# Group norm, keys and values of the next sequence inside the convolution, and weight transforms spread over attention, in a float32 attention-and-convolution kernel

## The chip, the cores and the metric

One core of one Trainium2 chip. The metric is device microseconds (us) of the whole program, the median of a kernel's runs. Engines: PE is TensorE, DVE is VectorE, ACT is ScalarE, POOL is GpSimd. A line number such as L311 belongs to the kernel whose profile is shown.

## The reference

Two layers over an input of 4 x 128 x 64 x 64 in float32. Only the first is touched by the change:

```python
def conv_layer(x):                       # x: (4, 128, 64, 64), each image is one "sequence"
    x = group_norm(x, 32)                # no scale, no shift
    g, theta, phi = conv1x1(x, gw, gb), conv1x1(x, tw, tb), conv1x1(x, pw, pb)   # 64 channels each
    f = einsum('bcn,bcm->bnm', theta, phi) / sqrt(64)                          # 4096 x 4096 per image
    out = conv1x1(einsum('bcm,bnm->bcn', g, softmax(f)), ow, ob) + x
    return relu(conv7x7(x) + conv5x5(x) + conv3x3(x) + out + x)
# x = x + conv_layer(x); the second layer (selective scan both ways, then a recurrence) follows
```

## The kernel before

For each of the four sequences the kernel does the following, one after the other: statistics and group norm; queries, keys and values; attention; a convolution in which the 7x7, 5x5 and 3x3 kernels are merged into one and applied along the rows by a polynomial transform with four pairs of points. `strip` sums on VectorE prepare the transformed input (14 ahead of the first pair, six more for each of the three later points), TensorE multiplies with transformed weights `u`, VectorE combines each pair of products into the outputs. The 128 x 128 `gmean` product averages statistics over the channels of a group, so a norm costs a small chain: mean product, subtraction, variance product, reciprocal root on GpSimd, and a product for the key bias.

```python
nc.vector.tensor_reduce(bsum, bias, AX.X, ALU.add)          # the first thing asked of VectorE
...
for b in range(B):
    for j in range(NQ):
        nc.vector.bn_stats(st[:, j, :], tb[:, bass.ts(j, NC)])
    nc.vector.bn_aggr(mv, st)
    nc.tensor.matmul(pm, k.gmean, mv[:, 0:1], ...)           # mean of the group
    ...                                                      # gm, dm, qv on VectorE
    nc.tensor.matmul(pv, k.gmean, qv, ...)                   # variance of the group
    ...                                                      # rs on GpSimd, xp = (t - gm) * rs on VectorE
    for q in range(NQ):                                      # 8 blocks of 512 columns
        nc.tensor.matmul(pt, tw2, xp[:, rows, 3 : W + 3], ...)
        nc.vector.tensor_scalar(theta[:, bass.ts(q, NC)], pt, tb2, None, ALU.add)   # queries
        nc.tensor.matmul(pp, pw2, xp[:, rows, 3 : W + 3], ...)                      # keys
        ...
    # attention: 128 steps (8 blocks of 16): 2 score products, exp on ScalarE,
    # one addition to the denominator on VectorE, 2 value products
    if b == 0:
        ...conv_weights(...)                                 # the weight transforms
    for n, p in enumerate(POINTS):                           # 4 points, 2 products each, 2 halves
        ...                                                  # strip sums f (strided), xs = f0 +- p * f1
        for q in range(H // QR):
            pr = ps_f.tile(...)                              # two PSUM buffers
            for i in range(2):
                product(pr[:, i], 2 + 2 * n + i, xs[i], q)
            nc.scalar.copy(m, pr[:, 1])
            nc.vector.tensor_tensor(v, pr[:, 0], m, ALU.subtract)
            nc.vector.tensor_tensor(m, pr[:, 0], m, ALU.add)
            ...                                              # four more into the outputs
    # residual on VectorE
```

A scheduler sets the order of the instructions on each engine when the kernel is built. `InOrder` pins an instruction behind the one traced before it; what is not pinned goes where the scheduler finds it ready.

## Time and profile before

| | |
|---|---|
| median time | 3404.35 us (3396.66 to 3410.28, 3 runs) |
| span of the profiled run, granted clock | 3408.1 us, 0.949 |
| PE / DVE / ACT busy | 89% / 79% / 51% of the span |
| end of the first layer (last convolution product) | 1771.9 us |

I use three marks: the first score product of a sequence, the end of its plain 1x1 products (they open the convolution's pairs), and the last product of the first layer. From the 1x1 products to the next first score is called a **transition** below; it takes 135.9, 135.5 and 135.5 us here. From the first score to the 1x1 products is the **attention stretch**: 330.4 us in the first sequence and 292.8 in the three others.

The page's slices of the span show where PE is not full, and two of its groups (columns: line, engine, operation, output from input, forms, count; then busy us and mean ns; then idle us of the engine just before, and what ended most of it).

```profile
PE   5899989999899998999986889888988898888776
PEclk9999989999899999999997998899899999999888
...
L289 PE MATMUL pr<-x,u 128*128 128x512 f32 x896 | 386.3, 593 | 0.0
...
L301 DVE SCALAR_TENSOR_TENSOR f<-xp,f 128x1120 f32<-128x1120 f32 x88 | 192.0, 2192 | 1.0
```

The left half of the slices is the first layer: nines, with a dip at the start and at each transition. The products of the pairs (L289) never wait: 0.0 us idle ahead of 896 instructions.

### The profile page before, as it was taken

What the parts mean: (1) busy time and instruction counts of PE and PEld (TensorE: products, weight loads), DVE (VectorE), ACT (ScalarE), POOL (GpSimd) and SP (SyncE); (2) the same over time, 40 slices, a digit from 0 to 9 for tenths busy, and PEclk for the clock granted to TensorE, in tenths of its full rate; (3) what the DMA queues carried; (4) which work ended last, traced back from release to release, by engine and by line L of the source; (5) the groups of instructions that cost most, each with busy time, mean ns of one, the idle gap of its engine ahead of it and who ended that gap; (6) DMA issues with size and microseconds to landing.
All of it is one profiled execution on the core that took longest, in us unless ns stands there. A gap on an engine that the chain in (4) does not pass through costs nothing.

```text
span 3408.1 us, 44290 instructions
## 1 busy us (share of the span) xinstructions
PE 3021.9 (89%) x16048; PEld 1456.4 (43%) x16048; DVE 2692.6 (79%) x4528; ACT 1740.2 (51%) x3087; POOL 528.1 (15%) x735
## 2 busy tenths in 40 slices
PE   5899989999899998999986889888988898888776
PEld 2223333333333333333344556555655565555446
DVE  6987767778677786877856998898889888898755
ACT  2444104441044420444205776777677767777454
POOL 0000000000000000000001433243324332333310
PEclk9999989999899999999997998899899999999888
DMA  4000000000000000000002322322223333333002
GB/s 149 17 1 1 0 0 1 1 1 0 0 1 1 0 0 0 1 1 1 1 11 59 75 82 68 78 75 76 74 77 76 75 75 78 82 81 81 3 1 100
DMA packets 72004, 128.21 MB, mean 38 GB/s; under 512 B 16864, under 2 KB 19936, under 8 KB 70880
## 3 DMA queue, kind: packets, MB, share of 16 engines
q1 hardware_dynamic: 65696, 120.84, 13.3%
q10 hardware_dynamic: 6080, 4.44, 0.4%
q8 instruction: 129, 2.11, 0.3%
q14 instruction: 99, 0.81, 0.1%
HBM read 115.80 MB, written 9.44 MB: 37 GB/s over the span
## 4 chain that ended last, share of the span: by engine, by line
PE 55%; DVE 28%; ACT 5%; issue 4%; POOL 3%; DMA 3%; SPq 0%; ACTq 0%; DVEq 0%; POOLq 0%
PE pf L91 13%; PE acc L91 12%; PE pr L289 11%; DVE xx L763 6%; PE pc L289 3%; DVE bc L763 3%; DVE cbc L849 2%; ACT xx L91 2%; DVE y L886 2%; DVE xdd L842 2%; DVE xdt L842 2%; DMA cbc<-csd 2%; DVE den L233 1%; PE pys L866 1%; PE pj L901 1%
## 5 line engine op out<-in xcount | busy, mean ns | idle before, releaser
L229 ACT ACTIVATE ex<-pf 128x1024 f32<-128x1024 f32 x512 | 497.7, 1021 | 493.6 <-PE pf L91 462.9
L233 DVE TENSOR_TENSOR den<-den,ex 128x1024 f32<-128x1024 f32 x448 | 547.6, 1222 | 194.1 <-ACT ex L229 171.3
L91 PE MATMUL pf<-theta,phi 64*128 64x512 f32 x2048 | 517.3, 622 | 26.1 <-ACT ex L229 26.1
L91 PE MATMUL acc<-ex,gT 128*64 128x512 f32 x2048 | 505.3, 610 | 0.0
L289 PE MATMUL pr<-x,u 128*128 128x512 f32 x896 | 386.3, 593 | 0.0
L91 PEld LDWEIGHTS pf<-theta,phi 64*128 64x128 f32 x2048 | 176.0, 187 | 359.9 <-ACT ex L229 218.8
L91 ACT ACTIVATE cbc<-cbc,s 128x128 f32<-128x128 f32 x1024 | 312.9, 406 | 0.0
L91 PEld LDWEIGHTS acc<-ex,gT 128*64 128x64 f32 x2048 | 122.7, 136 | 348.3 <-issue 346.4
L289 PEld LDWEIGHTS pr<-x,u 128*128 128x128 f32 x896 | 170.0, 190 | 219.3 <-issue 216.0
L763 DVE SCALAR_TENSOR_TENSOR xx<-pj,cw,xx 128x509 f32<-128x509 f32 (+2 forms) x384 | 259.6, 736 | 0.4
L866 PE MATMUL pys<-cbc,xdt 128*64 128x128 f32 x2048 | 185.1, 302 | 81.5 <-DVE y L886 81.3
L91 POOL TENSOR_TENSOR rms<-rms,neghalf 128x2 f32<-128x2 f32 x128 | 113.0, 883 | 583.7 <-DVE rms L912 583.7
L330 ACT COPY m<-pr 128x512 f32<-128x512 f32 x32 | 18.7, 586 | 356.5 <-PE pr L289 356.5
L301 DVE SCALAR_TENSOR_TENSOR f<-xp,f 128x1120 f32<-128x1120 f32 x88 | 192.0, 2192 | 1.0
L91 ACT ACTIVATE cbc<-cbc 128x1536 f32<-128x1536 f32 x128 | 190.0, 1484 | 3.4
L91 POOL TENSOR_TENSOR y<-y,zs 128x512 f32<-128x512 f32 x128 | 163.3, 1276 | 147.3 <-DVE y L886 144.0
L866 PEld LDWEIGHTS pys<-cbc,xdt 128*64 128x64 f32 x2048 | 118.9, 145 | 148.0 <-DVE y L886 111.3
L776 PE MATMUL pj<-un,full 128*128 128x512 f32 x256 | 150.6, 695 | 33.3 <-DVE xx L763 18.3
L754 PE MATMUL pj<-un,full 128*128 128x512 f32 x256 | 147.9, 663 | 34.9 <-DVE xx L763 20.2
L91 ACT ACTIVATE xx<-pj,cb,cw 128x512 f32<-128x512 f32 x128 | 97.5, 773 | 148.5 <-DVE y L886 116.5
L177 POOL MEMSET xp<- 128x210 f32 x4 | 1.1, 273 | 1039.9 <-DVE f L301 1039.9
L901 PEld LDWEIGHTS pj<-wout,y 128*128 128x128 f32 x1024 | 133.4, 200 | 58.7 <-issue 46.7
(210 smaller groups left out, 4997.3 us busy)
## 6 DMA issues: line engine op xcount, KB each, us to landing
cbc<-csd SPq DMA_DIRECT2D x256, 256.0 KB, 4.3
cbc<-csd SPq DMA_DIRECT2D x256, 128.0 KB, 4.5
t<-in_x SPq DMA_DIRECT2D x3, 2048.0 KB, 12.1
out<-t SPq DMA_DIRECT2D x2, 2048.0 KB, 18.2
out<-t ACTq DMA_DIRECT2D x2, 2048.0 KB, 18.3
w<-in_w7t SPq DMA_DIRECT2D x3, 896.0 KB, 5.0
t<-in_x SPq DMA_DIRECT2D x4, 512.0 KB, 4.9
v<-in_w5t SPq DMA_DIRECT2D x2, 640.0 KB, 4.0
```

What stands on the lines that cost most here:

```text
L91: return self.tc.keep_in_program_order(getattr(self.engine, name)(*args, **kw))
L229: nc.scalar.activation(ex, pf, AF.Exp, scale=scale)
L233: nc.vector.tensor_tensor(den[q], exs[q, 0] if m == 1 else den[q], ex, ALU.add)
L289: nc.tensor.matmul(o, u[:, n, y, :], x[:, q * QR + y : q * QR + y + QR, :], start=(y == 0), stop=(y == 6 and odd is None),)
L301: nc.vector.scalar_tensor_tensor(f, strip(i + 2 * j), cs[j], f, ALU.mult, ALU.add)
L754: pe.matmul(pp, full[:, d, DI + h * P : DI + (h + 1) * P], own(un, d, g), start=True, stop=True)
L763: vec.scalar_tensor_tensor(x[:, o:], self.pp[i][:, 0 : MG - o], cw[:, i, tap : tap + 1], x[:, o:], ALU.mult, ALU.add)
L776: pe.matmul(pz, full[:, d, h * P : (h + 1) * P], cols, start=True, stop=True)
L842: vec.tensor_tensor(x, px, self.r[f][:, :, self.c, :].unsqueeze(3).to_broadcast(heads), ALU.mult)
L849: vec.tensor_tensor(self.lt, self.lt, self.gm.unsqueeze(2).to_broadcast([P, ND, NHEAD, P]), ALU.mult)
L866: pe.matmul(o, self.xdt[:, d, h, :], self.lt[:, d, h, :], start=True, stop=S is None)
L901: pe.matmul(po[:, bass.ts(d, P)], self.y[:, d, h, :], wout[:, d, h, :], start=(h == 0), stop=(h == 1))
```

## The change

Its intent: fill the gaps between sequences and the ragged first attention. (1) The sum of the biases moves from the very start to behind the first attention. (2) The weight transforms become a generator, one step of which is taken per attention step. (3) The next sequence's statistics are issued ahead of the pairs of the convolution, its norm, keys and values inside the last pair, the first half of its queries behind the first half of the last pair, and the second half inside its attention. (4) Queries are evicted by ScalarE instead of VectorE.

```diff
-        nc.vector.tensor_reduce(bsum, bias, AX.X, ALU.add)
-        ...                                       # matmul with gb, add
-        pe = InOrder(tc, nc.tensor)
+        pe, vec = InOrder(tc, nc.tensor), InOrder(tc, nc.vector)
...
-                nc.vector.bn_stats(st[:, j, :], tb[:, bass.ts(j, NC)])
+                vec.bn_stats(st[:, j, :], t[:, ds(b * T + j * NC, NC)])
...
-                nc.vector.tensor_scalar(theta[:, bass.ts(q, NC)], pt, tb2, None, ALU.add)
+                nc.scalar.activation(theta[:, bass.ts(q, NC)], pt, AF.Identity, bias=tb2)
...
-                    nc.vector.tensor_tensor(den[q], exs[q, 0] if m == 1 else den[q], ex, ALU.add)
+                    vec.tensor_tensor(den[q], exs[q, 0] if m == 1 else den[q], ex, ALU.add)
+                next(beside, None)                # one step of the weight transforms
...
+                if n == NT // 4:
+                    theta += [queries(xp, h) for h in range(1, NH)]
...
+            after = statistics(b + 1) if b + 1 < B else None
             for n, p in enumerate(POINTS):
...
+                last = n == len(POINTS) - 1
+                if last and after:
+                    gm, rs, km = after
+                    xp = normalise(b + 1, gm, rs)
+                    phi, gT = keys(xp, km)
                 for h in range(NH):
...
+                    if last:
+                        ...                       # residual of this half
+                        if after and h == 0:
+                            theta = [queries(xp, 0), theta[1]]
...
+            for _ in range(32):
+                next(weights)
+            ...
+            attention(0, xp, theta, phi, gT, vec, weights)
+        vec.tensor_reduce(bsum, bias, AX.X, ALU.add)
```

Small parts left out here: the division of a block is split into three steps at different places, the check on the denominators takes sums by ScalarE instead of a maximum by VectorE, and the inputs of the later sequences are requested behind the first weights.

## The prediction

> **What bounds the kernel now.** I read the page's slices first: TensorE (PE) is at 89% of the span, and the convolution layer, which alone is changed, ends near 1772 us. Then the table of busy time by stretch, for layer 0 (columns: stretch, its length, busy us and instructions of PE, weight loads, VectorE, ScalarE, GpSimd, then granted clock, DMA share, GB/s).
>
> ```profile
> 61.80:486.60 424.80, 399.45 (x1342) 134.35 (x1338) 341.21 (x358) 149.07 (x178) 0.94 (x4) 0.98 0.03 8
> 530.40:915.20 384.80, 384.56 (x1330) 132.79 (x1330) 277.54 (x226) 136.55 (x142) 0.94 (x4) 1.00 0.00 1
> ...
> 915.09:956.38 41.29, 24.45 (x168) 10.87 (x166) 40.81 (x37) 9.84 (x20) 0.55 (x1) 0.79 0.00 1
> ```
>
> A sequence from its first score product to its last convolution product is PE bound: 384.6 of 384.8 us at clock 1.00. Three places are not. The first sequence takes 424.8 us for the same work (A). It starts only at 61.8 us (B). Between sequences lie 41.29 us (C), three times, in which VectorE is busy 40.81 us. The timelines say why. B: VectorE runs in order, and the first thing asked of it is the sum of four tiny biases.
>
> ```profile
> 12.08 0.69 DVE L158 BATCH_NORM_STATS2 st<-t 128x6 f32<-128x512 f32 x1 [1.50 <-DMA t<-in_x]
> ...
> 29.94 0.16 DVE L146 TENSOR_REDUCE bsum<-bias 128x1 f32<-128x4 f32 x1 [17.05 <-DMA bias<-in_ob]
> ...
> 33.99 2.42 DVE L181 TENSOR_SCALAR xp<-t,gm,rs 128x4096 f32<-128x4096 f32 x1 [0.76 <-POOL rs L80]
> ...
> 61.82 1.99 PE L91 MATMUL pf<-theta,phi 64*128 64x512 f32 x8
> ```
>
> C: the queries' evictions (0.75 us) stand in VectorE's order between strip sums (2.17 us), and PE waits for each.
>
> ```profile
> 932.89 2.17 DVE L301 SCALAR_TENSOR_TENSOR f<-xp,f 128x1120 f32<-128x1120 f32 x1
> 933.05 0.50 PEld L201 LDWEIGHTS pt<-xp,tw 128*128 128x128 f32 x2 [4.29 <-DVE theta L202]
> 933.05 2.08 PE L201 MATMUL pt<-xp,tw 128*128 128x512 f32 x2 [2.72 <-DVE theta L202]
> ```
>
> A: the weight transforms and 14 strip sums stand between the additions to the denominator; ScalarE waits for these additions (its buffers come free by them) and PE for ScalarE.
>
> ```profile
> 151.67 1.29 DVE L233 TENSOR_TENSOR den<-den,ex 128x1024 f32<-128x1024 f32 x1
> 152.80 2.22 DVE L301 SCALAR_TENSOR_TENSOR f<-xp,f 128x1120 f32<-128x1120 f32 x1
> 153.05 1.02 ACT L229 ACTIVATE ex<-pf 128x1024 f32<-128x1024 f32 x1 [2.19 <-PE pf L91]
> 154.13 2.08 PE L91 MATMUL pf<-theta,phi 64*128 64x512 f32 x4 [1.13 <-ACT ex L229]
> ```
>
> [...] 0.50 from 920 to 935 us inside gap C, 1.00 once dense; [...] after waits of 2.2 and 3.1 us near 123 and 102 us eight products took 3.66 and 3.50 us instead of 1.94. [...] Here the last bias took 18.3 us to land while 8 MB of input were under way.
>
> **The change, part by part.** Unit times from the trace: a convolution product (two records) 0.858 us, a step of attention 1.92 us of PE (4+4 records of 0.24), a denominator addition 1.17 us from start to start, a strip sum 2.12, an x combination 1.25, a reciprocal 3.26, one statistics instruction 0.63, a post-processing of one pair of products 5.4 (two of 0.7, four of about 1.0), a weight step 0.35 (five in 1.76).
>
> *Start.* The bias sum moves behind the first attention. The last input piece lands at 12.1; two statistics to 13.4; the chain that took 3.26 us (30.73 to 33.99) and one 0.2 us operation more bring the normalisation to 17.0, and 2.4 more to 19.4 (36.4 before). Eight key products with two ScalarE evictions of 0.48 each and some weight scalings between them pace at about 1.3 us[...]: 32; values 4 to 35; four query products 38.7. The first score product comes 23.1 us earlier. VectorE does its first 32 weight steps (about 12 us) in this shadow. In the built order the later inputs are requested behind the first weights, the third weight block near 32 us, so I expect it by 38, before it is needed near 43.
>
> *First attention.* Removed: the clump of weight steps. By the built order about 90 of them lie one per attention step: per 16 steps VectorE needs 15x1.17 + 0.6 + 3.26 + 0.6 + 15.5x0.35 = 27.4 us, PE 16x1.92 + 0.86 = 31.6. That fits; I allow 5 us of hiccups, since ScalarE's scalings wait for VectorE in order. But then, as the strip buffers open when the weight buffers close, the order puts 14 strip sums and 8 statistics between 15 denominator additions, in the sixth and seventh query block: 14x2.12 + 8x0.63 + 15x1.15 + 2x3.26 + 2 = 60 us of VectorE for 31.6 of PE. Four exp buffers cover about 4 us, so some 24 to 25 us of PE wait remain. Four query products are moved in: 3.4 us and 2 for ScalarE to evict them. Sum 5 + 25 + 5.4 = 35.4, against the 37.6 lost now (424.8 less 387.2, the latter with first products included). Gain 2.2.
>
> *Each transition.* On PE nothing goes away: 8 key, 8 query products and the values, 17.7 us, move into the last products or the next attention. The idle part of gap C is 41.3 - 17.7 = 23.6. What takes its place? VectorE's strip sums must still be done, and the order shows where. (1) A tiny product for the variance stands two products after the convolution's 1x1 part, but its operand is made after all strips: PE gets there at 821.8 on the old time axis, VectorE at 826.8. 5 us, 0.9 for the small products, 1.5 for half clock. (2) The next sequence's 14 strip sums (29.7 us) now lie between the post-processings, six of them in one block of 12.7 us before the third and again before the fifth. Two PSUM buffers: PE may begin pair k+2 only when VectorE has read pair k. Laying both orders side by side from pair 1 at 838.5: pair 5 waits 2.3, pair 6 1.2, pair 7 4.4: 8 us. (3) Queries wait for the first half's outputs: 1.5 us; values' evictions 1. So the next first score product is at 947.2 instead of 956.4, 9.2 earlier. (4) It pays 3.4 for the four queries moved into attention and about 3.5 because their eviction on ScalarE waits for the second half to be finished. Net 2.3, three times: 7.
>
> *Small ones.* The row maximum (0.68) leaves VectorE for a ScalarE copy with sum, 8 query evictions also; neither engine bounds attention (1.02 of 1.92 on ScalarE). The second layer's order on VectorE is unchanged: no effect.
>
> *Sum.* 23 + 2 + 7 = 32 us of 3404: about 3372. Since every piece of my reading that is uncertain was rounded to the dear side, I say 3366.
>
> **The rivals.** First, the intent comes off: PE never starves, transitions lose 23.6 each less about 5, attention of the first sequence all of its 37.6: 23 + 33 + 56 = 112, so 3292. For it: VectorE's mean is only 277.5 of 384.8 us, so there is room for 30 us more per sequence if it is spread well. Against: the order is fixed when built, and strip sums are clumped where their buffers come free. Second, the gap closes but returns as waits on two PSUM buffers and on the variance product (my reading), 3366. Third, worse: these waits of 4 to 5 us each drop the clock for several us and first attention, with ScalarE waiting for VectorE and VectorE for ScalarE, loses 20 us more: 3400 or slightly above. The clock after gap C stayed at half for some 10 us, which speaks for it; that PE stays mostly busy between these short waits speaks against.
>
> **Range and chances.** Start is sure to about 3 us. First attention may be off by 15 to either side, each transition by 5, three times the same way. That gives 3335 to 3390. Runs of before spread by 14. Faster by over 2% means below 3336: it needs most of rival one, 0.15. Slower by over 2% needs every transition to lose 20 us: 0.03.
>
> **What would show it.** Right if: the first score product lies near 39 us; a stretch of some 60 us late in the first attention has VectorE at 100% and PE at half, with strips between denominator additions; in each convolution a wait of about 5 us for the variance product, then waits of products for VectorE's subtraction or addition of an earlier pair; sequences repeat at about 426 us where they took 428.3. Wrong if: the repeat is under 415 (waits 1 and 2 absent), or the first sequence shows PE above 95% (strips harmless), or the first score product is later than 45 us (a weight or input transfer holds ScalarE).

No term of the sum goes with them: it stays at 23 + 2 + 7 = 32 us, so 3372, given as 3366. Two parts that concern the clock are estimates. The 32 us at which the key products end has some 2 us for a slow beginning (19.4 + 8 x 1.3 is 29.8): in the kernel before, the first three products of 512 columns behind the norm (at 36.97, 38.81 and 40.52 us) took 2.05, 1.91 and 1.63 us and later ones 1.04 to 1.15. That the clock is the cause there is not shown; the granted clock reads 1.00 from 36 to 42 us. The 1.5 us for half clock are near what a slow stretch took from eight records in the kernel before: 1.56 us at 103.4 and 1.67 at 123.6 (score records usually take 1.99).

What the kernel before shows of the rest, by its timeline and its table by stretch: VectorE held to its order at the start, as the eighth statistics instruction, whose input had landed by 12.1 us, ran at 30.01 behind the bias sum (at 11.66 in e1, where that sum is moved). The 0.50 and 1.00 of gap C are granted clock: 0.50 from 920 to 935 us, around and behind PE's wait of 9.67 us and with PE at work from 926.1, and 1.00 from 940 us on, where waits of 0.6 to 0.74 us remain. Behind the wait of 3.12 us at 102.3 it was 0.50 to 0.57 from 103.4 to 106.8, behind 2.21 us at 123.6 it was 0.50 to 0.55 up to 127.2, and 1.00 after each. ScalarE's wait for a denominator addition was 4.38 us at 149.84, and PE's wait for ScalarE behind it 2.41. From 0 to 30 us, while the last bias was landing, the DMA share was 0.88 at 319 GB/s.

## The result, and the profile after

| | before | after |
|---|---|---|
| median of the same rounds | 3407.32 us (3396.66 to 3415.02, 4 runs) | 3362.19 us (3355.72 to 3369.16, 4 runs) |
| ratio | | 0.987, 95% interval 0.9836 to 0.9905 |
| span of the profiled run, clock | 3408.1 us, 0.949 | 3367.4 us, 0.948 |
| end of the first layer | 1771.9 us | 1725.8 us |

A ratio is the mean time of one kernel's runs over that of the other's of the same rounds, so not quite the ratio of the medians. The change is faster by 1.3%, within 2%. The first layer lost 46.1 us; the second one, whose instructions keep their order, took 1636.2 us of the one span and 1641.6 of the other. Over all kernels below that rest lies between 1624.6 and 1641.6 us, with no relation to the edits that I can see. So the end of the first layer is the sharper measure, and I judge by it.

Start and first attention after, from the timeline and from the table by stretch (columns of the timeline: start, us, engine, line, operation, count, and in brackets the idle time before it and what ended it; the table's columns are those that the prediction names).

```profile
16.35 2.41 DVE L185 TENSOR_SCALAR xp<-t,gm,rs 128x4096 f32<-128x4096 f32 x1
...
38.78 1.99 PE L91 MATMUL pf<-theta,phi 64*128 64x512 f32 x8
```

```profile
38.80:230.00 191.20, 184.90 (x755) 55.95 (x754) 148.18 (x188) 103.22 (x132) 0.00 (x0) 1.00 0.02 6
230.00:290.00 60.00, 45.05 (x164) 12.61 (x162) 59.59 (x46) 20.64 (x23) 0.00 (x0) 0.89 0.00 0
370.45:484.95 114.50, 107.54 (x367) 48.32 (x365) 82.34 (x80) 17.77 (x32) 0.60 (x2) 0.99 0.00 0
786.20:911.87 125.67, 114.35 (x376) 51.47 (x374) 86.80 (x83) 17.37 (x32) 1.49 (x5) 0.96 0.00 0
1212.90:1332.24 119.34, 112.31 (x376) 50.84 (x375) 82.28 (x74) 17.60 (x32) 1.49 (x5) 0.97 0.00 0
```

The norm is applied at 16.4 us instead of 34.0, the first score comes at 38.8 instead of 61.8. The weight transforms hardly disturb attention up to 230 us (PE busy 184.9 of 191.2). Then come 60 us with VectorE full and PE at 45.05: strip sums and statistics among the denominators. The last three rows are the transitions, and the surprise is in their lengths: three transitions of the same code differ by up to 11 us. About 5 of them are only a shift: 17 records of the pairs (the profile lists a float32 product as two: the 448 products of the pairs are its 896 records) lie ahead of the first transition, five ahead of the others, and twelve at 0.43 us are 5.1. The PE waits tell the rest. First the products for the variance of the next sequence, PE and then VectorE:

```profile
371.55 0.28 PE L166 MATMUL pv<-qv,gmean 128*128 128x1 f32 x2
791.35 0.59 PE L166 MATMUL pv<-qv,gmean 128*128 128x1 f32 x2 [4.53 <-DVE qv L164]
1218.33 0.59 PE L166 MATMUL pv<-qv,gmean 128*128 128x1 f32 x2 [4.58 <-DVE qv L164]
```

```profile
786.44 4.34 DVE L300 SCALAR_TENSOR_TENSOR f<-xp,f 128x1120 f32<-128x1120 f32 x2
790.70 0.15 DVE L160 COPY gm<-pm 128x1 f32<-128x1 f32 x1
...
791.08 0.22 DVE L164 SCALAR_TENSOR_TENSOR qv<-dm,mv 128x1 f32<-128x1 f32 x1
```

In the second and third transition the 0.15 us copy of the mean stands behind the last strip sums, which end near 790.7; PE has been waiting since 786.8. In the first transition the strip sums were done during the long first attention, so nothing waits. Second, the pairs:

```profile
444.27 1.83 PE L311 MATMUL pr<-x,u 128*128 128x512 f32 x2 [3.93 <-DVE m L354]
...
871.22 2.04 PE L311 MATMUL pr<-x,u 128*128 128x512 f32 x2 [3.96 <-DVE m L354]
...
1267.40 24.27 PE L311 MATMUL pr<-x,u 128*128 128x512 f32 x56 [0.70 <-ACT m L351]
```

```profile
845.52 4.94 DVE L91 BATCH_NORM_STATS2 st<-t 128x6 f32<-128x512 f32 x8
```

A wait of about 3.9 us stands in the first two transitions (with 0.7 and 0.4 us in two earlier pairs) and not in the third, where 0.70 is the only one. At 845.5 us VectorE makes eight statistics between two pairs. They are those of the sequence after the next, brought forward by the scheduler, and the six strip sums of the predicted clump (856.9 to 869.5 us) come behind them; in the third transition there is no such sequence any more, and with its strip sums alone PE waits 0.70 us. The page sums it up, where the group showed 0.0 idle before:

```profile
L311 PE MATMUL pr<-x,u 128*128 128x512 f32 x896 | 398.8, 601 | 10.9 <-DVE m L354 8.7
```

The books of the first layer, by first score products (us):

| kernel | first score | sequence 1 to 2 | 2 to 3 | 3 to 4 | 4th to end | end of layer | median of program | ratio to before, 95% |
|---|---|---|---|---|---|---|---|---|
| before | 61.8 | 466.3 | 428.3 | 428.3 | 387.2 | 1771.9 | 3407.32 | |
| after | 38.8 | 446.2 | 426.9 | 420.4 | 393.6 | 1725.8 | 3362.19 | 0.987 (0.9836, 0.9905) |
| e1_bias_late | 43.4 | 466.4 | 429.0 | 428.2 | 387.2 | 1754.2 | 3395.52 | 0.9973 (0.9952, 0.9995) |
| e2_queries_scalar | 60.0 | 460.6 | 421.8 | 421.3 | 387.2 | 1750.8 | 3390.77 | 0.9957 (0.9937, 0.9977) |
| e9_two_lines | 42.5 | 462.5 | 421.4 | 421.9 | 387.2 | 1735.4 | 3374.78 | 0.9898 (0.9875, 0.9921) |
| e3_old_transition | 37.8 | 456.4 | 435.4 | 433.6 | 396.2 | 1759.5 | 3390.04 | 0.996 (0.9941, 0.9978) |
| e11_unfolded | 38.4 | 447.5 | 425.8 | 417.6 | 391.1 | 1720.4 | 3359.54 | 0.986 (0.9834, 0.9886) |
| e4_few_strips_first | 37.9 | 434.6 | 425.8 | 419.8 | 393.6 | 1711.7 | 3349.02 | 0.9844 (0.982, 0.9869) |
| e5_stats_early | 38.5 | 440.0 | 417.5 | 417.6 | 395.2 | 1708.8 | 3347.96 | 0.9814 (0.9785, 0.9843) |
| e6_strips_beside | 37.7 | 440.2 | 422.2 | 422.9 | 395.8 | 1718.8 | 3358.41 | 0.9848 (0.9819, 0.9877) |
| e7_both | 38.0 | 440.5 | 419.5 | 420.4 | 397.5 | 1715.8 | 3354.09 | 0.9836 (0.98, 0.9873) |
| e8_first_spread | 37.8 | 443.3 | 422.5 | 420.5 | 395.9 | 1719.9 | 3355.18 | 0.9839 (0.9806, 0.9871) |
| e10_chain_spread | 38.5 | 441.4 | 412.8 | 412.8 | 393.6 | 1699.1 | 3335.33 | 0.978 (0.9761, 0.9799) |
| e12_first_too | 38.5 | 450.1 | 414.4 | 412.7 | 393.6 | 1709.3 | 3341.96 | 0.9802 (0.9779, 0.9825) |

Medians come from different chips; the ratios are against the kernel before on the same chip. The end of the layer is read from one profiled run of each kernel. Of the program times that were expected below, all but e10's were too low, by 2 to 33 us. All runs gave correct results but e4.

### The profile page after: what moved, and what is told of

The parts are those of the page before. It is cut to its first block, busy times and chain, and to the rows that moved or that the text cites. A ratio compares the mean times of both kernels' runs of the same rounds, so it can differ in the third digit from the quotient of the medians.

```text
span 3367.4 us, 44357 instructions
## 1 busy us (share of the span) xinstructions
PE 3030.2 (90%) x16048; PEld 1468.6 (44%) x16048; DVE 2652.3 (79%) x4464; ACT 1784.1 (53%) x3183; POOL 529.7 (16%) x735
## 4 chain that ended last, share of the span: by engine, by line
PE 50%; DVE 34%; ACT 5%; issue 5%; POOL 3%; DMA 1%; SPq 0%; DVEq 0%; POOLq 0%; ACTq 0%
PE pf L91 12%; PE acc L91 12%; PE pr L311 8%; DVE xx L846 5%; DVE bc L846 3%; DVE f L300 3%; DVE cbc L932 2%; DVE den L91 2%; ACT xx L91 2%; DVE y L969 2%; DVE xdt L925 2%; DVE xdd L925 2%; PE pj L753 1%; DVE f L298 1%; DVE theta L358 1%
## 5 line engine op out<-in xcount | busy, mean ns | idle before, releaser
L311 PE MATMUL pr<-x,u 128*128 128x512 f32 x896 | 398.8, 601 | 10.9 <-DVE m L354 8.7
L837 PE MATMUL pj<-un,full 128*128 128x512 f32 x256 | 149.8, 670 | 31.8 <-DVE xx L846 19.9
## 6 DMA issues: line engine op xcount, KB each, us to landing
out<-t SPq DMA_DIRECT2D x2, 2048.0 KB, 18.4
```

The lines of the kernel that those rows point to most:

```text
L311: nc.tensor.matmul(o, u[:, n, y, :], x[:, h * QR + y : h * QR + y + QR, :], start=(y == 0), stop=(y == 6 and att is None),)
L837: pe.matmul(pp, full[:, d, DI + h * P : DI + (h + 1) * P], own(un, d, g), start=True, stop=True)
```

## The experiments

The theory after reading the traces: the start gains because a wait for a late transfer leaves VectorE's order; the transitions gain what VectorE no longer does there, and give some of it back as waits on small things that stand behind long ones in VectorE's order. The main rival: the place of the products, inside the convolution, is what gains.

### Parts of the change put into the kernel before

**e1_bias_late**, the bias sum alone:

```diff
-        nc.vector.tensor_reduce(bsum, bias, AX.X, ALU.add)      # at the start, with its product and addition
+            (the same three instructions behind the attention of sequence 0, VectorE's two pinned there)
```

> The kernel before with one edit: the sum of the biases is issued behind the first attention. My theory, that the wait for the bias transfers alone held VectorE back at the start: the first score product moves from 61.8 us to between 43 and 46 (the queries are still evicted by VectorE, so not quite the 38.8 of the changed kernel), the rest of the layer stays as before (repeats of 428.4 us), and the time is about 3390 us, 17 us under the kernel before. The rival, that the start gained because keys and queries were taken off VectorE and regrouped: the first score product stays within 5 us of 61.8 and the time within 6 us of the kernel before.

The first score moved to 43.4 us, 18.4 earlier, and the layer's end by 17.7; later repeats stayed at 428 to 429. For the start the theory stands. The program's time fell by only 7.9 us in the same rounds (3403.41 to 3395.52), not by 17; behind the layer this kernel's profiled run took 1641.5 us and that of the kernel before 1636.2, and the rest of the difference stays open. The 4.6 us from here to the changed kernel's 38.8 are what its other edits at the start give.

**e2_queries_scalar**, the queries' eviction alone:

```diff
-                nc.vector.tensor_scalar(theta[:, bass.ts(q, NC)], pt, tb2, None, ALU.add)
+                nc.scalar.activation(theta[:, bass.ts(q, NC)], pt, AF.Identity, bias=tb2)
```

> The kernel before with one edit: ScalarE adds the bias to the queries and evicts them, instead of VectorE; nothing is moved into the convolution. My theory, that part of what a transition gained is simply work taken off VectorE, which is busy 40.8 of the 41.3 us between the last product of the convolution and the first score product: the stretch from the end of the 1x1 products to the next first score product falls from 135.8 to about 128 us, three times, and the time to about 3383 us. The rival, that only the move into the products gains: that stretch stays within 2 us of 135.8 and the time within 6 us of the kernel before.

Transitions fell to 128.8, 129.0 and 128.5 us, 6.5 to 7.1 each, and the layer's end by 21.1 (the program's time by 12.6 in the same rounds, from 3403.41 to 3390.77). Before and with this line, the end of a transition on PE:

```profile
944.22 1.14 PE L201 MATMUL pt<-xp,tw 128*128 128x512 f32 x2 [0.72 <-DVE theta L202]
...
952.50 3.95 PE L215 MATMUL pg<-gw,xp 128*64 128x64 f32 x128 [0.74 <-DVE theta L202]
```

```profile
936.04 1.04 PE L201 MATMUL pt<-xp,tw 128*128 128x512 f32 x2
937.24 1.14 PE L204 MATMUL pp<-xp,pw 128*128 128x512 f32 x2 [0.17 <-ACT phi L207]
938.32 4.13 PE L215 MATMUL pg<-gw,xp 128*64 128x64 f32 x128
```

The waits of 0.7 us for VectorE, one per block of queries, are gone. The strip sums stay on VectorE, and PE no longer waits for it behind them.

The largest wait of a transition is another one, and this line leaves it. In the kernel before PE waits 16.8 us in all from the last 1x1 product to the next first score, and 9.7 of them at the product for the key bias, whose operand `mx` stands behind the last combinations, the norm and the residual on VectorE (9.65 us in e2). In the changed kernel the whole chain comes early. Before, then after:

```profile
926.11 0.59 PE L190 MATMUL pk<-mx,pw 128*128 128x1 f32 x2 [9.67 <-DVE mx L188]
```

```profile
373.00 0.35 PE L174 MATMUL pk<-mx,pw 128*128 128x1 f32 x2 [0.21 <-DVE mx L172]
```

**e9_two_lines**, both edits together:

```diff
+ (the edits of e1 and e2)
```

> The kernel before with two small edits and none of the reordering: the bias sum behind the first attention, and the queries evicted by ScalarE. The two runs with one edit each took 17.6 and 21 us off the end of the layer (1771.9 us). Theory, that the two add up and that the rest of the change is about even by itself: first score product at 40 to 43 us, transitions 129 us, attentions 293 us, end of the layer at 1729 to 1736 us against 1725.8 of the changed kernel, the time about 3370 us. The rival, that they share a gain: end of the layer at 1745 us or later.

The layer ended at 1735.4 us, 36.5 of the change's 46.1 us, and inside the expected band; the program took 3374.78, a little above the 3370 expected. Two edits of a line or so carry four fifths of what the whole change gains in this layer. The remaining 9.6 us are the sum of gains and losses that the next runs separate.

### Parts of the change taken back

**e3_old_transition**: norm, keys and first queries back behind the convolution.

```diff
-            after = statistics(b + 1) if b + 1 < B else None
+            after = None
...
+                gm, rs, km = statistics(b)       # in the loop, behind convolve of b - 1
+                xp = normalise(b, gm, rs)
+                phi, gT = keys(xp, km)
+                theta = [queries(xp, 0)]
```

> The changed kernel with normalise, keys and the first half of the queries back behind the convolution, and everything else (start, weights beside attention, queries by halves on ScalarE) as changed. If the move into the last products is what gained: the stretch from the 1x1 products to the next first score product goes back to 132 us or more, the sum of a transition and an attention to about 428, and the time to about 3386 us. My theory, that the move is nearly paid back by the waits it makes and the work put behind the first scores: the sum of a transition and an attention is 421 to 425 us (mean of the changed kernel 420.3, before 428.4), and the time 3366 to 3376 us.

My numbers were missed: 1759.5 us, and transition and attention stretch together took 429.5 to 433.8 us, more than before the change. But the edit did more than I meant. The statistics are pinned in the changed kernel, so that once they stood behind the residual, PE waited for them:

```profile
905.74 0.59 PE L158 MATMUL pm<-mv,gmean 128*128 128x1 f32 x2 [13.76 <-DVE mv L156]
...
911.01 6.34 PE L198 MATMUL pp<-xp,pw 128*128 128x512 f32 x8 [1.74 <-DVE xp L185]
```

So the run agrees in its size with the rival and yet does not test it. It shows the cost of statistics at the wrong place.

**e11_unfolded**: only the products go back; statistics and norm stay inside the convolution.

```diff
-                if last and after:
-                    gm, rs, km = after
-                    xp = normalise(b + 1, gm, rs)
-                    phi, gT = keys(xp, km)
...
-                        if after and h == 0:
-                            theta = [queries(xp, 0), theta[1]]
+            if after:                             # behind all pairs
+                gm, rs, km = after
+                xp = normalise(b + 1, gm, rs)
+                phi, gT = keys(xp, km)
+                return xp, [queries(xp, 0)], phi, gT
```

The normalising has no pin, and the built order still has it inside the convolution on VectorE.

> The changed kernel with only the products of the keys, the values and the first queries put back behind the products of the convolution on TensorE; the statistics and the normalising stay inside the convolution. The earlier run that put all of it back also put the statistics behind the residual, which made the mean product wait 13.8 us, so it was no fair test. Theory, that what the fold gains is that the normalised input is ready early, and not that the products stand between others: transitions within 4 us of the changed kernel's 114.3, 126.1 and 119.6, end of the layer at 1724 to 1738 us. The rival, that the place of the products is the gain: each transition 8 us or more longer, end of the layer at 1750 us or later.

The layer ended at 1720.4 us, below the expected band and 5.4 earlier than with the products inside. Transitions grew by 1.3 to 3.1 us (115.6, 129.2, 121.0), attention stretches shrank by 2.6 to 4.2 (to 296.6). Behind the last pair PE goes on without a wait:

```profile
895.27 1.92 PE L198 MATMUL pp<-xp,pw 128*128 128x512 f32 x4
897.35 6.50 PE L198 MATMUL pp<-xp,pw 128*128 128x512 f32 x12 [0.16 <-ACT phi L201]
903.90 4.00 PE L209 MATMUL pg<-gw,xp 128*64 128x64 f32 x128
```

So the rival falls: the place of the products inside the convolution gains nothing. That statistics and norm are made early, so that the normalised input is ready when the last pair ends, is enough.

### The waits that the change made

**e5_stats_early**: the next sequence's statistics beside the attention of sequences 1 and 2 (counted from 0), one per three attention steps; the small chain follows at once.

```diff
-            after = statistics(b + 1) if b + 1 < B else None
+            if b == 0:
+                after = statistics(1)
...
+        def beside(b, xp, box, made):
+            for _ in range(24):
+                yield
+            if b + 1 < B:
+                yield from every(3, statistics_steps(b + 1, box))
```

> The changed kernel with the statistics of the next sequence made one by one beside the attention, in sequences 1 and 2 (sequence 0 as it is). Theory: the 4.5 us wait for the variance product comes from the small chain of the statistics standing behind strip sums on VectorE, and the 3.9 us wait in the seventh pair from eight statistics placed among the pairs; both vanish. Transitions of 114.5, 126.2 and 119.7 us become about 110, 114 and 112; attention stays at 299 to 301; the time falls by about 23 us to 3339. The rival, that the next wait in line (strip sums on VectorE) takes over: transitions shrink by less than 2 us each and the time stays within 6 us of 3362.

Both waits vanished, and the transitions were 107.9, 112.0 and 111.9 us, within 2.1 of what was expected. But the attention stretches of these two sequences grew from 300.8 to 305.5 and 305.7, so the layer ended at 1708.8 and not at 1703. The timeline shows where:

```profile
579.00 0.38 PE L167 MATMUL pv<-qv,gmean 128*128 128x1 f32 x2 [0.86 <-DVE qv L165]
580.51 0.59 PE L175 MATMUL pk<-mx,pw 128*128 128x1 f32 x2 [1.14 <-DVE mx L173]
581.03 2.08 PE L91 MATMUL pf<-theta,phi 64*128 64x512 f32 x4
```

The three one-column products stand in PE's order, each waits for the link before it on another engine, and behind them four score records take 2.08 us instead of 1.13. From 570 to 590 us the granted clock was 0.83. The query block in which this happens took 37.9 us in one sequence and 36.4 in the next, where all its neighbours took 31.5.

**e10_chain_spread**: the same, with the chain's links three attention steps apart and pinned there.

```diff
             pm = ps_c.tile([P, 1], F32, tag="c", name="pm")
-            nc.tensor.matmul(pm, k.gmean, mv[:, 0:1], start=True, stop=True)
+            pe.matmul(pm, k.gmean, mv[:, 0:1], start=True, stop=True)
+            yield
             gm = wk.tile([P, 1], F32, tag="gm", name="gm")
...
+            (a yield between all further links as well)
```

> The run with early statistics, with the small chain of each statistics (mean, variance, reciprocal root, key bias: three products of one column on TensorE, and the small steps between them) spread over the attention, three attention steps between two links, so that no product of the chain waits for VectorE or GpSimd. Theory: of the 4.8 us that each attention grew in that run, the chain's waits and the half clock behind them are all but the eight statistics; attentions of sequences 1 and 2 go from 305.6 back to 300 to 302, transitions stay at 108, 112 and 112, the end of the layer comes at 1698 to 1702 us instead of 1708.8, the time about 3338. The rival, that the statistics' own 5 us of VectorE time is the cost: the attentions stay at 305.

Attention stretches of 300.9, transitions of 107.8, 111.9 and 111.9, end of the layer at 1699.1: all as the theory said. One reservation: the two query blocks that hold statistics and chain still took 31.8 and 32.9 us, 1.7 more than usual. The stretch is not longer than the changed kernel's because its first denominator product came 45.8 us behind the first score and not 47.4: the records behind its wait of 1.78 us at 903.2 took their usual 1.13 and 1.94 us, where those behind 1.76 us in the changed kernel took 2.04 and 2.67. Spreading and pinning were not tried apart. One wait of the chain is left, and the clock of its surroundings is 1.00 (the second line is the stretch of 40 us around it):

```profile
597.30 0.38 PE L91 MATMUL pv<-qv,gmean 128*128 128x1 f32 x2 [0.53 <-DVE qv L91]
```

```profile
590.00:630.00 40.00, 39.47 (x165) 12.36 (x166) 30.11 (x29) 20.06 (x24) 1.53 (x1) 1.00 0.00 1
```

With 3335.33 us and a ratio of 0.978 (0.9761 to 0.9799) this version beats both kernels.

**e6_strips_beside**: the 14 opening strip sums of sequences 1 to 3 spread over attention, statistics as in the change.

```diff
-                attention(b, xp, theta, phi, gT, nc.vector, iter(()))
+                attention(b, xp, theta, phi, gT, vec, beside(b, xp, box, made))
...
+            yield from every(5, first_strips(xp, made))
```

> The changed kernel with the 14 strip sums that open a convolution spread over the attention before it, in sequences 1 to 3; the statistics stay where they are. Theory: the waits in the fifth, sixth and seventh pair (0.7, 0.4 and 3.9 us) vanish, since VectorE gets ahead of TensorE, but the wait of 4.5 us for the variance product stays, since later strip sums stand ahead of it: transitions 110, 121 and 119 us, the time 3350 to 3356. The rival, that lighter VectorE work also removes the variance wait: transitions 110, 114 and 112, the time about 3339. If the strip sums disturb the attention instead, the attention grows from 300 by over 5 us each and the time exceeds 3365.

The waits in the pairs vanished as expected, transitions were 106.9, 120.8 and 121.1, and the variance product's wait stayed and grew. But this run moves more than strip sums: with the additions pinned (`vec`), the statistics can no longer be brought forward into the pairs; they stand at 749.7 us, ahead of them. So it doesn't tell which of the two the pairs had waited for. The wait that grew:

```profile
789.07 0.58 PE L166 MATMUL pv<-qv,gmean 128*128 128x1 f32 x2 [6.96 <-DVE qv L164]
```

Less work on VectorE did not help the variance product, since the scheduler put the strip sums of a later point where the first ones had been. It is a matter of order and not of load.

**e7_both**: e5 and e6 together.

```diff
+            if b + 1 < B:
+                yield from every(3, statistics_steps(b + 1, box))
+            yield from every(5, first_strips(xp, made))
```

> Statistics and strip sums both beside the attention, in sequences 1 to 3. Theory: no wait over 1 us is left in the products of the convolution, transitions of about 109, 112 and 111 us, attention 299 to 302, the time about 3337. The rival, that VectorE's work beside attention delays the additions of the denominators: attention over 305 us each and the time 3350 or more.

Transitions came as expected (106.9, 110.9, 110.9), but attention took 308.6, 309.5 and 303.1 us: in this half the rival was mostly right, and the run was worse than e5 by 7 us at the layer's end. It isn't the strip sums alone: in e6 they were spread over the same attention, and it took 301.4 to 301.9. In e7 the block with the unspread chain is again the longest (37.3 and 38.2 us for 31.5), and behind it three denominator products wait 0.7 to 1.6 us each, 3.5 in all, as the strip sums delay the denominators' sums. They buy only 1 us per transition once the statistics are out of the way.

### The first attention

**e4_few_strips_first**, a wrong result: 4 strip sums instead of 14 in the first sequence.

```diff
-            m = len(cs) - 1
+            m = 1 if few else len(cs) - 1         # few: sequence 0, opening strips
```

> The changed kernel, with a wrong result on purpose: in the first sequence each of the strip sums ahead of the first point is one instruction instead of three or four, so 4 of them stand where 14 stood. My theory, that these sums hold up the additions of the denominators on VectorE and with them the first attention: first score product to the end of the 1x1 products falls from 331.7 us to between 309 and 318, and the time to about 3344 us; the later sequences are unchanged. The rival, that the stretch lost is TensorE's clock or ScalarE's exponentials: 331.7 stays within 4 us.

The stretch of the first attention fell from 331.9 to 320.5 us, more than the rival allowed and less than I expected. Ten sums of 2.12 us were taken away and 11.4 us gained: about half a microsecond of PE for each of VectorE. The same 60 us as shown above:

```profile
230.00:290.00 60.00, 52.54 (x210) 15.59 (x208) 48.47 (x44) 25.74 (x29) 0.00 (x0) 0.94 0.00 1
```

**e8_first_spread**: e7, and in the first sequence the statistics and opening strips one per two attention steps behind the weight transforms.

```diff
+            yield from weights
+            scratch.__exit__(None, None, None)    # then the strip buffers may be opened
+            yield from every(2, statistics_steps(1, box))
+            yield from every(2, first_strips(xp, made))
```

> As the run with both, and in the first sequence too the statistics and the opening strip sums are spread, one per two attention steps, behind the last weight transform. Theory: VectorE has 282 us of work in the 332 us from the first score product to the end of the 1x1 products, so spread evenly it need not hold TensorE: that stretch falls from 331.7 to between 312 and 320 us, and the time to about 3322 us, which would be more than 2% under the kernel before. The rival, that the stretch is bound by VectorE whatever the order: it stays within 4 us of 331.7, and the time is that of the run with both.

330.6 us: no gain. It is a loss, as only one record of the pairs lies in this stretch where the changed kernel has 17: from the first score to the next sequence's it took 443.3 us, and 440.5 in e7. The unspread chain cost PE here what it cost in e5 and more (columns as above; the four score records behind it took 2.08 us instead of 1.13 and the eight value records 2.51 instead of 1.94):

```profile
260.13 0.38 PE L159 MATMUL pm<-mv,gmean 128*128 128x1 f32 x2 [3.82 <-DVE mv L157]
262.34 0.59 PE L167 MATMUL pv<-qv,gmean 128*128 128x1 f32 x2 [1.83 <-DVE qv L165]
264.01 0.59 PE L175 MATMUL pk<-mx,pw 128*128 128x1 f32 x2 [1.08 <-DVE mx L173]
```

I took these 6.7 us and the slow products behind them for the cause of the miss.

**e12_first_too**: e10, and the first sequence spread too; its chain has one attention step between two links, not three as in e10.

```diff
+            yield from every(1, statistics_steps(1, box, pe, vec))
+            yield from every(2, first_strips(xp, made))
```

> As the run with the spread chain, and in the first sequence as well: statistics and spread chain of sequence 1, then the opening strip sums, one per two attention steps, behind the weight transforms. In the earlier run that spread them with an unspread chain, the chain's waits (3.8, 1.8 and 1.1 us and the half clock behind them) ate the gain. Theory: from the first score product of sequence 0 to that of sequence 1 it falls from 440 us (early statistics alone) to between 430 and 436 us, the end of the layer comes at 1690 to 1697 us, the time about 3330. The rival, that VectorE bounds that stretch: 439 us or more, end of the layer no earlier than in the run with the spread chain.

The theory fell: from the first score to the next sequence's it took 450.1 us, 8.7 more than in e10. The chain's products still waited 2.30, 2.04 and 0.59 us, so the closer links are part of it. And where the strip sums begin, VectorE has no pause any more, while PE waits for the denominators' sums (a row of the table by stretch and a line of the timeline):

```profile
264.15:297.09 32.94, 25.91 (x100) 7.75 (x98) 32.38 (x23) 12.55 (x14) 0.00 (x0) 0.86 0.00 1
```

```profile
292.59 2.07 PE L91 MATMUL pd<-den,ones 128*128 128x512 f32 x2 [7.03 <-DVE den L91]
```

The mean load had misled me (282 us of VectorE work in 332). An estimate of what fits in: from the unit times in the prediction a block of 16 steps has 31.5 us of PE and needs 15 x 1.17 + 0.6 + 3.26 + 0.6 = 22.0 us of VectorE. That leaves 9.5 us, four strip sums; one per two steps are eight, 17.0 us. The weight transforms end with 37 of the 128 steps left, so about 22 us are free, and the 14 sums and eight statistics need 34.7. By this estimate spreading over what is left of the attention cannot hide them; the weight transforms would have to end earlier, which I did not try.

## Why the prediction was right or wrong

The time was predicted as 3366 us and came as 3362.19; "faster by over 2%" had been given 0.15 and did not come. The sum was less exact than that, and that the total came so near is partly luck. It said 32 us, rounded up to 38; the first layer gave 46.1. Point by point:

- **Start: right.** 23.1 us predicted, 23.0 measured, norm at 16.4 us (17.0 predicted). e1 gives 18.4 of them to the bias sum.
- **First attention: right in size and place, the mechanism half confirmed.** 35.4 us of loss were predicted. The stretch is 39.1 over the 292.8 of an undisturbed one; but PE had already done the twelve records of the pairs, 5.1 us. That leaves 34.0. The stretch of 60 us with VectorE full is there. PE is busy for 75% of it and not half. The blocks of 31.5 us in it took 45.6 and 38.5, so 21.1 us against the predicted 24 to 25; e4 confirms that ten of the 14 strip sums make half of that, the rest (statistics among them) was not isolated.
- **Transitions: the mis-sized term.** The prediction has "net 2.3, three times: 7". Measured: transitions shortened by 21.6, 9.4 and 15.9 us, the later attention stretches lengthened by 8.0, 8.0 and 6.4, together 24.5, or 19.4 without the 5.1 that belong to the first attention. What was wrong is "three times", and the size of the pairs' wait. I had laid the order of one transition side by side with the old one and multiplied. In us, predicted and measured:

| term | predicted, each | first | second | third |
|---|---|---|---|---|
| wait for the variance product | 5 | 0 | 4.5 | 4.6 |
| half clock, (1 - granted clock) x the time in which PE works | 1.5 | 1.7 | 4.1 | 2.2 |
| pairs waiting for VectorE | 8 | 5.1 | 5.1 | 0.7 |
| queries | 1.5 | 1.7 | 1.7 | 1.7 |

  Predicted three times, these terms are 48.0 us; measured they are 33.1. Of these 14.9 us 1.7 go to the next point (22.4 us paid later, 20.7 predicted), and what is left is near the 12.4 by which the transitions' net gain exceeded 7. (Two further terms of the prediction, 0.9 for small products and 1 for the values' evictions, I did not isolate.) e5 and e10 show that both waits hang on the place of the statistics: with them moved, all three transitions take 108 to 112 us. For the variance product that is the predicted wait. For the pairs it is not: the prediction gave its 8 us to the strip sums alone, and with the statistics gone and these sums still there (the third transition, where the scheduler also places them a little differently, and e5) the pairs wait 0.70 to 0.75 us. The clock's share was too small in the second transition.
- **What the transition pays later: right.** 6.9 us predicted (3.4 and 3.5), 8.0, 8.0 and 6.4 measured. All of the 8 us lie ahead of the first denominator product, which comes 47.4 us behind the first score instead of 39.4; the query blocks behind it take 31.5 in both kernels. The four queries there take 4.2 us, and the rest is a wait of 1.75 us for the exponentials, with slow products behind it in the first two cases. The cause is the predicted one: on ScalarE the first eviction waits for the residual of the second half, and the exponentials stand behind it.

```profile
920.63 0.69 ACT L223 ACTIVATE theta<-pt,tb 128x512 f32<-128x512 f32 x1 [3.30 <-DVE t L362]
```

- **The intent, "the intent comes off" at 3292: rightly given little.** Filling the gap with products gained nothing (e11); by the traces what helped there is that statistics and norm are made early. (The sum of this rival is also off: it says "all of its 37.6" and adds 33.) Taking the queries off VectorE gave 21.1 us by itself (e2). The prediction has that move only among the small ones, as a matter of engine load. I had read the waits of gap C for the queries and not drawn the conclusion that one line removes them, and I had not named its largest wait, the 9.7 us of the key-bias product.

That the first attention stretch grew by 4.6 us in e1 (330.4 to 335.0) while the first transition shrank by 4.4 is a shift: ten more records of the pairs lie ahead of its 1x1 products. Open: whether e10 with the products left outside as in e11 is faster still; how much each of statistics and remaining strip sums costs in the first attention.

## What to carry to other kernels

Filling a gap pays only what the busy engine was really waiting for: try first to take the small, in-order operations that it waits for off the engine that is full, which here was one line for 21 us. When work is folded into another stage, look at where its small dependent links land in each engine's order, and put several steps of other work between two links; unspread, three products of one column and eight statistics lengthened a query block by 5 to 6 us. And count a loss in each repetition separately, since the first and the last have other neighbours.

## What the traces show besides

- PE's clock behind a wait. Behind a wait of 1.76 us at 922.3 us in the changed kernel the granted clock was 0.52 to 924 us and 0.56 to 926; four score records took 2.04 us instead of 1.13 and the next eight value records 2.67 instead of 1.94. It was not so each time: behind 1.74 us at 488.9 in e5 the same instructions took 1.13 and 1.94. No run tests what makes the difference.
- VectorE and the step of its operands. In the changed kernel strip sums, which read every fourth element (128x1120), took 2.19 us each (median), and the three-operand combination of the same size and type from contiguous operands 1.32. With 512 elements the combinations into the outputs, which read and write at that step, took 1.10 us, and the contiguous residual 0.68. No run changes the step alone.
- A short chain across engines inside a dense stream of products, e5 against e10: with three one-column products of 0.4 to 0.6 us close together (and eight statistics before them) the query block took 6.4 and 4.9 us more than usual; with three attention steps between the links, two blocks together took 1.7 us more.
